# A state-space scan on one core: the output products of a group's third and fourth token block move to the projections' PSUM banks

## The chip, the cores and the metric

The kernel runs on one core of a Trainium2 chip. The metric is the device time of one execution in microseconds (us). A core has five engines with a queue of their own each: TensorE (PE in the profile, its weight loads PEld), VectorE (DVE), ScalarE (ACT), GpSimd (POOL) and SyncE (SP), which here issues the DMAs. TensorE writes its results into PSUM, which has eight banks of 2 KB for each of the 128 partitions; a tile of 128x512 numbers of 32 bits fills one bank.

## What is computed

The reference is one layer of a network on 16 sequences of 32 tokens with 512 features: a graph part, a scan part (a selective state-space layer of 128 heads in 8 groups), and a feed-forward part. The change lies in the scan part, whose reference is, cut to its core:

```
proj = einsum('bsd,od->bso', h, in_proj_w)
gate = proj[..., :D_INNER]                       # D_INNER = 8192
hBC  = silu(causal_conv(proj[..., D_INNER:...], conv_w, conv_b))
...
y  = (Y_diag + Y_off) + Dp * hid
yg = y * silu(gate)
ygr = yg.reshape(b, s, 8, 1024)
ygr = ygr * rsqrt(mean(ygr * ygr, axis=-1) + EPS)
out = einsum('bsd,od->bso', ygr.reshape(b, s, D_INNER) * gnorm_w, out_proj_w)
return residual + out
```

The 512 tokens are four blocks of 128. The 8192 inner features are eight groups of 1024, and a group is eight tiles of 128 features.

## The kernel before

The scan part (`scan_part`) holds the normalised input transposed as `hT` and goes through the groups with four functions.

- `project(t)` loads 256 KB of `in_proj` into one of six `win` buffers (L1117) and makes one 128x512 product in four matmuls of 128x128 weights (L1120), in a PSUM tile of the pool `ps_p`, tag "p". This pool has two banks, used in turn.
- `inner(g)` does this for the eight tiles of a group, twice each: the gate, `ppg`, which ScalarE's Silu carries to `gs` (L1199), and the features, `ppch`, which `convolve` carries to `hid` with one ScalarE and three VectorE instructions on the PSUM tile (L1127, L1132) and a Silu (L1135). `gs` and `hid` have two buffers each, so the projections of group g+2 write where group g's values were.
- `mix(g)` does the scan within the group, tile by tile: transposes of `hid` into `pht` (L1228), scaled by VectorE to `hd` (L1230); decays from GpSimd, TensorE and ScalarE (`da`, `pl`, `ed`, L1208 to L1218); VectorE's products `el` (L1241); the matmuls `py` (L1249); VectorE's `hid` and `gs` (L1253, L1254); ScalarE's squares and scaling (L1256 to L1261), with GpSimd adding the squares to `ssq` (L1260).
- `close(g)` ends the group. Four small matmuls `pn` sum `ssq` (L1268); from them ScalarE and VectorE make the factor `rs` (`gr` in the profile). The eight tiles `wo` of `out_proj` are loaded (L1276, ten buffers). Then, for each of the four token blocks q, eight matmuls with a 128x512 result add up in `po` (L1281), and VectorE reads `po`, scales it by `rs` and adds it to `xt` (L1284).

The eight banks are four pools of two: `ps_p` (projections), `ps_m` (`pht`, `pl`), `ps_y` (`py`, `pn`) and `ps_o` (`po`):

```
ps_p = cx.enter_context(tc.tile_pool(name="sps_p", bufs=2, space=PSUM))
ps_m = cx.enter_context(tc.tile_pool(name="sps_m", bufs=2, space=PSUM))
ps_y = cx.enter_context(tc.tile_pool(name="sps_y", bufs=2, space=PSUM))
ps_o = cx.enter_context(tc.tile_pool(name="sps_o", bufs=2, space=PSUM))
```

A pool hands its banks out in the order in which the program asks for tiles, and the first write to a tile waits until the last reader of the tile that had the bank before is done. The program asks in this order: `inner(0)`, `inner(1)`, `mix(0)`, `close(0)`, `inner(2)`, `mix(1)`, `close(1)`, and so on. The order within each engine's queue isn't the order of the text. The framework's scheduler builds it ahead of time and lets instructions that it holds for ready go before older ones that aren't. So in the built kernel the output products of the first two blocks are spread over the mix of their group, as tiles of `gs` become ready; the products of the last two follow after `pn`; and between a mix's instructions there are also the first projections of the group after the next. On TensorE, the end of group 3 in the built order reads (a number behind x counts matmuls):

```
pn3 x4, po3_0 x1, po3_1 x2, po3_2 x8, po3_3 x8, ppch40 x2, pht32 x3, ppg41 x4, ppch41 x4, ...
```

Here `ppg40` and half of `ppch40`, the first projections for group 5, stand further up, in the mix of group 3.

Of the kernel before, what the change touches and what calls it, by code (L numbers as in the profile page):

```python
# [8 lines left out]
F32 = mybir.dt.float32  # L9
# [9 lines left out]
P = 128  # L19
B = 16  # L20
C = 32
D = 512
# [1032 lines left out]
def scan_part(nc, tc, cx, I, id32, ones, xt, u, rstd, lows):  # L1055
# [6 lines left out]
# [4 lines that stand above are left out]
# [198 lines left out]
    def close(g, gs, ssq):  # L1264

        pn = ps_y.tile([P, 4], F32, tag="y", name=f"pn{g}")
        for q in range(4):
            nc.tensor.matmul(pn[:, q:q + 1], lhsT=ssq[:, q * P:(q + 1) * P], rhs=ones[:, 0:1], start=True, stop=True)  # L1268
        mean = sm.tile([P, 4], F32, tag="gm", name=f"gm{g}")
        nc.vector.tensor_scalar(mean, pn, 1.0 / (TG * P), None, ALU.mult)  # L1270
        rs = sm.tile([P, 4], F32, tag="gr", name=f"gr{g}")
        rstd(sm, rs, mean, 4, f"gn{g}")
        wo = []
        for i in range(TG):
            w = wpool.tile([P, D], F32, tag="wo", name=f"wo{g}_{i}", bufs=TG + 2)
            nc.sync.dma_start(out=w, in_=I["out_proj"][g * TG + i])  # L1276
            wo.append(w)
        for q in range(4):
            po = ps_o.tile([P, D], F32, tag="o", name=f"po{g}_{q}")
            for i in range(TG):  # L1280
                nc.tensor.matmul(  # L1281
                    po, lhsT=gs[:, i, q * P:(q + 1) * P], rhs=wo[i], start=(i == 0), stop=(i == TG - 1)
                )
            nc.vector.scalar_tensor_tensor(xt[:, q], po, rs[:, q:q + 1], xt[:, q], ALU.mult, ALU.add)  # L1284

    cur = inner(0)
    for g in range(G_M):
        nxt = inner(g + 1) if g + 1 < G_M else None
        ssq = mix(g, *cur)
        close(g, cur[0], ssq)  # L1290
        cur = nxt
# [142 lines left out]
```

## Time and profile before

| what | us |
|---|---|
| three runs | 2415.48, 2420.97, 2423.53 |
| their median | 2420.97 |
| the profiled execution's own time | 2416.21 |
| span of its trace | 2414.5 |
| TensorE busy | 2190.0 |
| VectorE busy | 1699.6 |
| matmuls of `po` (L1281), busy | 240.5 |
| matmuls of `ppg` and `ppch` (L1120), busy | 231.9 and 232.2 |
| VectorE's readout of `po` (L1284), mean of one | 0.748 |

The span runs from the first to the last instruction of the trace, and the profiled execution's time has 1.7 us around it. Busy times of TensorE are modelled ends of pipelined matmuls, so neighbours overlap by some 0.17 us in the rows and the distance of two starts tells more than a duration. A program's matmul with 32-bit operands leaves two records in the trace. The output products lie between 1586 and 2315 us; the feed-forward part follows, and starts with the layer norm of `xt`.

### The profile page before, as it was taken

The page shows a single profiled execution, that of the slowest core. Times are in us where ns is not written, and L with a number is a line of the kernel's source. Part 1 is how long each engine was busy: PE and PEld are TensorE (multiplying, and loading weights), DVE is VectorE, ACT ScalarE, POOL GpSimd, SP SyncE. Part 2 cuts the span into 40 slices and gives each one's busy share as a digit, 9 for nine tenths or more (in the row PEclk, how much of TensorE's full clock was granted, in tenths as well). Part 3 has the DMA queues.
Part 4 walks back from the last instruction along what each step waited for, and adds up shares of the span by engine and source line. Part 5 has one row for each costly group of instructions (what it writes and reads, how often), then busy time and mean ns, then how long its engine had stood idle before and what let it go on. Part 6 is the DMA issues. An engine that isn't in the chain of part 4 may idle for free. (4 is left out here: it accounts for less than half of the span.)

```text
span 2414.5 us, 88867 instructions
## 1 busy us (share of the span) xinstructions
PE 2190.0 (91%) x39234; PEld 1248.1 (52%) x39234; DVE 1699.6 (70%) x3674; ACT 1100.1 (46%) x2023; POOL 831.6 (34%) x897
## 2 busy tenths in 40 slices
PE   5699798999999778789999789999999999999979
PEld 2255455667676454567777544444444444444422
DVE  8487797888899888889999866554553625446643
ACT  6677566667665334345555322333332424333331
POOL 2165556445446565664655300020210202021200
PEclk9799899999999999999999899999999999999989
DMA  1323232132132231422211212213112121210000
GB/s 48 80 55 77 48 80 57 43 73 47 36 70 56 54 77 46 91 52 65 63 34 41 91 53 77 75 32 91 53 53 71 35 91 46 73 55 20 27 36 18
DMA packets 121625, 137.99 MB, mean 57 GB/s; under 512 B 18398, under 2 KB 79506, under 8 KB 121154
## 3 DMA queue, kind: packets, MB, share of 16 engines
q1 hardware_dynamic: 121240, 132.32, 21.9%
q8 instruction: 308, 5.05, 0.9%
q14 instruction: 77, 0.63, 0.1%
HBM read 77.02 MB, written 12.85 MB: 37 GB/s over the span
## 5 line engine op out<-in xcount | busy, mean ns | idle before, releaser
L849 POOL TENSOR_TENSOR EN<-e,rz 128x480 f32<-128x480 f32 x344 | 342.4, 995 | 554.4 <-DVE rz L847 430.1
L874 PE MATMUL u<-WA,DD 128*32 128x128 bf16 (+1 forms) x16512 | 418.6, 250 | 26.4 <-issue 26.4
L874 PEld LDWEIGHTS <-DD 128*32 128x32 f16 x16512 | 338.8, 98 | 72.7 <-issue 68.5
L879 ACT COPY us<-u 128x512 f32<-128x512 f32 x516 | 302.0, 587 | 149.5 <-PE u L874 131.8
L834 ACT ACTIVATE e<-s,smc 128x480 f32<-128x480 f32 x344 | 227.6, 662 | 290.7 <-PE s L829 248.0
L770 POOL TENSOR_TENSOR DD<-fs,crep 128x480 f16<-128x480 f32 (+2 forms) x344 | 349.6, 1017 | 0.0
L902 PEld LDWEIGHTS h<-e,us 128*32 128x32 f32 (+1 forms) x11008 | 248.8, 126 | 144.1 <-issue 65.6
L902 PE MATMUL h<-e,us 128*32 128x30 f32 (+1 forms) x11008 | 282.0, 211 | 37.1 <-DVE e L855 19.4
L821 DVE TENSOR_REDUCE c<-s 128x16 bf16<-128x480 f32 x344 | 220.7, 642 | 107.0 <-PE s L812 104.4
L1132 DVE SCALAR_TENSOR_TENSOR cyh<-ppch,t_conv_w,cyh 128x496 f32<-128x496 f32 (+2 forms) x192 | 137.4, 716 | 221.7 <-ACT cyh L1127 217.7
L1208 POOL TENSOR_TENSOR da<-lei,dA 128x512 f32<-128x512 f32 x32 | 40.6, 1269 | 611.8 <-PE pl L1213 577.5
L1281 PE MATMUL po<-wo,gs 128*128 128x512 f32 x512 | 240.5, 605 | 10.4 <-DVE xt L1284 10.3
L1120 PE MATMUL ppch<-hT,winch 128*128 128x512 f32 x512 | 232.2, 593 | 0.0
L1120 PE MATMUL ppg<-hT,wing 128*128 128x512 f32 x512 | 231.9, 593 | 0.0
L855 DVE STREAM_TRANSPOSE e<-EN 128x512 f32<-128x512 f32 x344 | 224.4, 652 | 0.0
L841 DVE TENSOR_REDUCE z<-e 128x16 f32<-128x480 f32 x344 | 219.5, 638 | 0.0
L539 ACT ACTIVATE sgn<-kd 128x512 bf16<-128x512 f32 x256 | 153.0, 598 | 56.2 <-PE kd L538 52.4
L812 PEld LDWEIGHTS <-DD 128*32 128x32 f16 x5504 | 81.7, 96 | 163.2 <-issue 129.5
L723 DVE TENSOR_SCALAR oh<-it,rank 128x512 bf16<-128x512 f16 x512 | 158.0, 368 | 7.5 <-PE pp L689 7.5
L812 PE MATMUL s<-DX,DD 128*32 128x120 f16 x5504 | 143.1, 223 | 19.6 <-DMA DX<-DD 16.2
L1120 PEld LDWEIGHTS ppch<-hT,winch 128*128 128x128 f32 x512 | 93.7, 190 | 122.7 <-issue 122.3
L1120 PEld LDWEIGHTS ppg<-hT,wing 128*128 128x128 f32 x512 | 95.8, 190 | 114.0 <-issue 114.0
(327 smaller groups left out, 2845.6 us busy)
## 6 DMA issues: line engine op xcount, KB each, us to landing
DX<-DD SPq DMA_DIRECT2D x456, 90.0 KB
wo<-in_out_proj SPq DMA_DIRECT2D x64, 256.0 KB
wing<-in_in_proj SPq DMA_DIRECT2D x64, 256.0 KB
winch<-in_in_proj SPq DMA_DIRECT2D x64, 256.0 KB
crep<-dC SPq DMA_DIRECT2D x128, 64.0 KB
dS<-so SPq DMA_DIRECT2D x32, 256.0 KB
fs<-dS SPq DMA_DIRECT2D x128, 64.0 KB
wincB<-in_in_proj SPq DMA_DIRECT2D x8, 256.0 KB
```

The lines of the kernel that those rows point to most:

```text
L770: nc.gpsimd.tensor_tensor(d[:, :, m0 - n0:n1 - n0], win, crep[:, :, m0:n1].unsqueeze(3).to_broadcast([P, 4, n1 - m0, K]), ALU.subtract,)
L812: nc.tensor.matmul(s[rh, j * 4 * QB:(j + 1) * 4 * QB].rearrange("p (b q) -> p b q", b=4), lhsT=d[:, h, c0:c0 + 32], rhs=dx[:, h, :, c0:c0 ...
L821: nc.vector.tensor_reduce(c, live["s", at, gi].rearrange("p (i q) -> p i q", q=QB), AX.X, ALU.max, negate=True)
L834: nc.scalar.activation(e, s.rearrange("p (i q) -> p i q", q=QB), AF.Exp, scale=smc)
L841: nc.vector.tensor_reduce(z, e, AX.X, ALU.add)
L849: nc.gpsimd.tensor_tensor(en[:, :, :QB], e, rz.unsqueeze(2).to_broadcast([P, NI, QB]), ALU.mult)
L855: nc.vector.transpose(e.rearrange("p i q -> p (i q)"), en.rearrange("p i q -> p (i q)"))
L874: nc.tensor.matmul(u[rh, jj], lhsT=d[:, h, c0:c0 + 32], rhs=WA[k][:, h].rearrange("p b o -> p (b o)"), start=(jj == 0 and k == 0), stop=(k ...
L879: nc.scalar.copy(us[:, j - jj:j + 1], u)
L902: nc.tensor.matmul(h[r:r + co, pr, q0:q0 + QB], lhsT=us[:, j, b * co:(b + 1) * co], rhs=e[:, 4 * j + b, :QB], start=npair > 1, stop=True, ...
L1120: nc.tensor.matmul(pp, lhsT=w[:, k], rhs=hT[:, k], start=(k == 0), stop=(k == 3))
L1281: nc.tensor.matmul(po, lhsT=gs[:, i, q * P:(q + 1) * P], rhs=wo[i], start=(i == 0), stop=(i == TG - 1))
```

## The change

`close` takes the PSUM tiles of the third and fourth token block (q = 2, 3) from `ps_p` under the tag "p", in place of `ps_o` under "o". The first and second stay where they were. Nothing else is edited.

```
         for q in range(4):
-            po = ps_o.tile([P, D], F32, tag="o", name=f"po{g}_{q}")
+            pool, tag = ((ps_o, "o"), (ps_p, "p"))[q // 2]
+            po = pool.tile([P, D], F32, tag=tag, name=f"po{g}_{q}")
             for i in range(TG):
                 nc.tensor.matmul(
                     po, lhsT=gs[:, i, q * P:(q + 1) * P], rhs=wo[i], start=(i == 0), stop=(i == TG - 1)
                 )
```

Every line from L1280 on has a number that is one higher in the changed kernel, so `po`'s matmuls are L1282 and its readout is L1285 there. The scheduler builds the queues anew for the changed program. On TensorE the end of group 3 becomes

```
pn3 x4, po3_0 x1, po3_1 x2, po3_2 x8, po3_3 x8, ppg40 x4, ppch40 x4, ppg41 x4, ppch41 x4, ...
```

and no projection stands in a mix any more. In SyncE's queue one weight load of six groups (2 to 7), the seventh of the group, stands behind the eight `wo` loads in place of ahead of them.

More of the change, by code (lines that the diff above doesn't have):

```diff
@@ L1278, in close @@
         for q in range(4):
-            po = ps_o.tile([P, D], F32, tag="o", name=f"po{g}_{q}")
+            pool, tag = ((ps_o, "o"), (ps_p, "p"))[q // 2]
+            po = pool.tile([P, D], F32, tag=tag, name=f"po{g}_{q}")
             for i in range(TG):
```

## The prediction

> **What bounds the kernel now.** I read the page's engine totals first, then the scan's stretch of TensorE's timeline, then its waits, group by group.
>
> ```profile
> PE 2190.0 (91%) x39234; PEld 1248.1 (52%) x39234; DVE 1699.6 (70%) x3674; ACT 1100.1 (46%) x2023; POOL 831.6 (34%) x897
> ...
> L1281 PE MATMUL po<-wo,gs 128*128 128x512 f32 x512 | 240.5, 605 | 10.4 <-DVE xt L1284 10.3
> ```
>
> The columns of the second line are busy time, mean ns of one, and the idle time just before them with its releaser. TensorE (PE) is the busiest engine. One matmul of the program is two records here (256 output matmuls, x512). Eight records of a projection start 3.433 us after the eight before them, so a 128x512 matmul costs 0.858 us of TensorE when they follow each other. The wait that the change can reach is the 10.3 us behind `xt`.
>
> The stretches from the end of one group's output products to the end of the next one's (groups 0, 1, 2 to 5 together, 6 and 7):
>
> ```profile
> 1577.50:1631.46 53.96, 52.42 (x243) 26.30 (x243) 32.41 (x48) 19.34 (x27) 14.61 (x10) 1.00 0.11 34
> 1631.46:1735.09 103.63, 102.09 (x367) 48.01 (x366) 50.63 (x74) 36.38 (x52) 15.62 (x11) 1.00 0.21 61
> 1735.09:2155.43 420.34, 415.31 (x1473) 193.03 (x1472) 202.15 (x296) 146.72 (x208) 59.34 (x44) 1.00 0.20 60
> 2155.43:2260.56 105.13, 98.86 (x358) 46.51 (x357) 51.58 (x74) 35.32 (x51) 16.06 (x11) 1.00 0.15 44
> 2260.56:2315.51 54.95, 50.78 (x241) 24.72 (x239) 32.22 (x50) 16.18 (x24) 11.55 (x9) 1.00 0.02 6
> ```
>
> After the stretch's length come busy PE, weight loads, DVE, ACT, POOL, then the granted clock. Up to group 5 PE idles 1.3 to 1.5 us a group (length less busy PE); in group 6 it idles 6.3. Groups 2 to 5 take 420.34 / 4 = 105.09 each. Now the same for the mix alone, group 5 and group 6:
>
> ```profile
> 2205.54:2260.56 55.02, 48.75 (x239) 24.60 (x238) 35.78 (x52) 21.37 (x29) 16.06 (x11) 1.00 0.08 25
> 2100.49:2155.43 54.94, 53.70 (x250) 26.34 (x249) 34.62 (x52) 22.73 (x30) 14.87 (x11) 1.00 0.12 32
> ```
>
> Equal lengths, yet group 5 fits in 4.95 us more of PE work. TensorE's timeline of group 5 shows what that is, and the wait at the end:
>
> ```profile
> 2102.04 1.88 PE L1120 MATMUL ppg<-hT,wing 128*128 128x512 f32 x4
> ...
> 2105.51 1.12 PE L1120 MATMUL ppg<-hT,wing 128*128 128x512 f32 x2
> ...
> 2108.12 1.02 PE L1120 MATMUL ppg<-hT,wing 128*128 128x512 f32 x2
> ...
> 2110.59 1.88 PE L1120 MATMUL ppch<-hT,winch 128*128 128x512 f32 x4
> ...
> 2137.60 2.82 PE L1281 MATMUL po<-wo,gs 128*128 128x512 f32 x6
> 2141.59 14.00 PE L1281 MATMUL po<-wo,gs 128*128 128x512 f32 x32 [1.17 <-DVE xt L1284]
> ```
>
> Twelve records, six matmuls, are projections for group 7, run in group 5's mix while the mix waits for VectorE. Group 6 has no such work, because there is no group 8. Its waits:
>
> ```profile
> PE py L1249 <- DVE el L1241: 3.7, 6, 1.4
> PE po L1281 <- DVE xt L1284: 1.2, 1, 1.2
> PE pht L1228 <- DVE hd L1230: 0.8, 1, 0.8
> PE pn L1268 <- POOL ssq L1260: 0.4, 1, 0.4
> PE pht L1228 <- ACT ed L1218: 0.2, 1, 0.2
> ```
>
> **The change part by part.** No instruction's form or count changes. `po2` and `po3` of each group leave the two "o" banks for the two "p" banks. Three things follow.
>
> (1) *The wait before `po2` goes.* It came from `po0`'s bank, which is free only when the factor `rs` is there and VectorE has read the bank. By starts: group 5's six records from 2137.60 end at 2137.60 + 6 x 0.429 = 2140.17, the next starts at 2141.59: 1.42. Group 6: 1.43. Group 0: 2 records of `ppch16` from 1615.43, then 1617.62: 1.33. Group 7: 4 records from 2297.51, then 2301.51: 2.28. Sum 1.33 + 6 x 1.42 + 2.28 = 12.1 us gained, all on the path, since PE is the chain there. The "p" bank that `po2` takes is free: its last reader, the convolution of the last projection (L1132), ran at 2209.3 in group 6, 35 us earlier. The gain's lower bound is 0, if that bank were taken after all; its upper bound is the wait itself. I take the whole wait.
>
> (2) *The projections ahead leave the mix.* The "p" pool has two banks in turn. In program order `po2` and `po3` of group g now stand between the projections of group g+1 and those of g+2, so the first two projections of g+2 can't start until `po2` and `po3` are read out. In the changed kernel's instruction order they follow `po3`, all 16 in a row. What leaves the mixes: `ppg16` (4 matmuls) and three of `ppch16` in group 0, six matmuls in each of groups 1 to 5: 37. In the open stretch each costs 0.858: 37 x 0.858 = 31.7 us. What the mix gives back for it is what the rows say: with six of them 54.94, without 55.02, so nothing. Is group 6 a fair copy? In the changed kernel the instruction order of VectorE, ScalarE and GpSimd in groups 1 to 5 is that of group 6 before, instruction for instruction, and TensorE's is too but for three or four transposes (three cost 0.33) that now stand behind the projections. The cover was VectorE's work (35.78 of 55.02 busy, most in the first 40 us) and the chain `hd`, `el`, `py`; with the fillers gone PE idles there. In group 0 the first five fillers stood while `py1` waited for `hd` (until 1583.23), so that start doesn't move. From below: group 7's mix, without convolutions, runs 2260.56 to 2315.24, less its 2.28 wait 52.40, against 55.02 - 1.43 = 53.59 for group 6; if six mixes were like that, 6 x 1.19 = 7.1 less. From above: nothing beyond 31.7. I take 31.7, as group 6 is the nearer row, and keep 24.6 for the range.
>
> (3) *Two matmuls of `po2` go ahead.* In group 0 one stands where the sixth filler stood, in group 7 one before `pn7`, where PE idles 0.92 for `ssq`. 2 x 0.86 = 1.7 us gained; bounds 0 and 1.7.
>
> SyncE's queue: in six groups (2 to 7) the seventh projection-weight load moves behind the eight `wo` loads, because its buffer is freed by the first projection. It is now issued about 3.4 us after `po3` and needed six projections later, at 20.6: 17.2 us of lead. Before, the following load had 2157.34 to about 2174.6, also 17 us, with the same burst in front (2150 to 2160) and no wait. I cost it at nothing. Behind it stand only later weights. Banks at the seam: `po2`'s readout (2253.89, 0.75 long) ends 6 us before the first projection wants the bank, `po3`'s about 1 us after `po3`, wanted 3.43 after: nothing. The Silu that empties a projection waits for `po3` in both kernels.
>
> Sum: + 31.7 - 12.1 - 1.7 = **+17.9 us**. Check by boundaries: groups 2 to 6 would take 5 x (16 x 3.433 + 55.02 + 0.33 - 1.43) = 544.2 for 525.47 (+18.8), group 1 108.85 for 103.63 (+5.2), group 0 -3.05, group 7 -3.14: +17.8. The profiled execution would go from 2416.21 to 2434.1 (span 2414.5 to 2432.4). It is 4.76 below the median of the runs; on 2420.97 that is **2438.9 us**.
>
> [...]
>
> **The rivals.** (a) *The mixes shrink when the fillers go*, and only the removed waits count: 2421.0 - 13.8 = 2407. For it: PE is 91% busy and the wait is plain. It decides once each of six mixes is 17.9 / 6 = 3.0 us shorter than group 6's. Against: group 6's 5.1 us of waits for VectorE, GpSimd and ScalarE (the list above without `xt`), with the very order that the others now get.
> (b) *The mixes are like group 7's*: +17.9 - 7.1 = +10.8, 2431.8. For: group 6's start is crowded by the last convolution. Against: in the changed order that convolution stands there in every group.
> (c) *`po2` still waits*, the change doesn't do what it says: +31.7, 2452.7. Against: the 35 us above.
> (d) *The seam stalls*, a weight arriving late behind the `wo` burst: each us costs 6; by the whole burst of 10 us it is +60, near 2499. Against: 17 us of lead.
>
> **How the numbers follow.** Forecast 0.84, (a) 0.03, (b) 0.08, (c) 0.03, (d) 0.02. The runs of before spread from 2415.48 to 2423.53. Low end: fastest run + 10.8 = 2426.3, taken as 2427. High end: slowest run + 17.9, with group 0's 3.05 not gained, 2444.5, and 1.5 for rows that differ: 2446. A measurement of this kernel can tell a change of about 0.3% (7.3 us) from none. Faster by more: (a), 0.03. Within: the parts of (a) and (b) near zero, 0.03. Slower: the rest, 0.94.
>
> **What would show it.** The wait of `po` for `xt` gone from PE's list; `py` waiting for `el` some 3 to 4 us in each of groups 1 to 6; no projections inside a mix; 16 in a row after `po3` with no gap; groups 2 to 5 at about 108.9 us each, group 7 near 51.5. Wrong if those groups stay at 105 or less, if `po` still waits for `xt`, or if projections wait at the seam.

## The result, and the profile after

Six runs of the changed kernel took 2437.02 to 2446.91 us, median 2438.96; six of the kernel before took 2412.85 to 2423.53, median 2420.39. The ratio is 1.0091, with a 95% interval of 1.0068 to 1.0114: 22 us slower (16 to 28). The ratio uses every run; the two medians alone lie 18.6 us apart. The profiled execution took 2437.02 us with a span of 2435.3, which is 20.8 us more than the one of before. The prediction of 2438.9 us and of a slower kernel held, and so did the sum's two large terms. A small one, for the clock, was missing.

The page's totals and the line of the output products, with the columns as before:

```profile
PE 2194.5 (90%) x39234; PEld 1253.2 (51%) x39234; DVE 1700.7 (70%) x3674; ACT 1098.1 (45%) x2023; POOL 834.4 (34%) x897
...
L1282 PE MATMUL po<-wo,gs 128*128 128x512 f32 x512 | 240.8, 607 | 0.2 <-ACT gs L1261 0.2
```

Same work, same counts. The idle time before `po` fell from 10.4 us to 0.2, so the wait that the change was to remove is gone. The stretches from group to group, cut at the end of each group's output products (groups 0, 1, 2, 3, 5, 6, 7; then busy PE, weight loads, DVE, ACT, POOL, and the granted clock):

```profile
1575.42:1627.53 52.11, 48.30 (x229) 24.84 (x229) 31.73 (x48) 19.34 (x27) 13.78 (x10) 0.97 0.10 31
1627.53:1737.28 109.75, 105.25 (x369) 49.94 (x368) 50.01 (x74) 36.45 (x52) 15.38 (x11) 0.98 0.19 58
1737.28:1848.40 111.12, 106.62 (x369) 50.37 (x368) 50.01 (x74) 36.44 (x52) 15.37 (x11) 0.97 0.20 57
1848.40:1957.16 108.76, 103.71 (x369) 48.87 (x368) 51.48 (x74) 36.49 (x52) 15.86 (x11) 1.00 0.20 59
...
2065.94:2174.83 108.89, 103.83 (x370) 48.87 (x368) 51.46 (x74) 36.49 (x52) 16.07 (x11) 1.00 0.20 60
2174.83:2283.61 108.78, 103.73 (x369) 48.82 (x368) 51.46 (x74) 35.20 (x51) 16.07 (x11) 1.00 0.15 43
2283.61:2335.16 51.55, 50.27 (x241) 24.80 (x239) 32.24 (x50) 16.18 (x24) 11.56 (x9) 1.00 0.02 7
```

A group lasts 108.8 us at full clock, where it lasted 105.1, and PE now idles 5.1 us in it (108.76 less 103.71) where it idled 1.3. Groups 1 and 2 are longer still, and there the clock isn't 1.00. The waits on PE over the scan, summed (us in total, times, longest):

```profile
PE py L1249 <- DVE el L1241: 21.9, 36, 1.4
PE pht L1228 <- DVE hd L1230: 4.7, 6, 0.8
PE py L1249 <- DVE hd L1230: 3.3, 1, 3.3
PE pn L1268 <- POOL ssq L1260: 2.8, 7, 0.4
```

In the kernel before, the first of these was 4.9 us, 10 times, most of it in group 6. The waits of group 6 now stand in each mix of groups 1 to 6. The seam, on PE's timeline at the end of group 5:

```profile
2158.44 16.55 PE L1282 MATMUL po<-wo,gs 128*128 128x512 f32 x38
2174.83 3.60 PE L1120 MATMUL ppg<-hT,wing 128*128 128x512 f32 x8
2178.26 3.60 PE L1120 MATMUL ppch<-hT,winch 128*128 128x512 f32 x8
```

All 38 records of the rest of `po` in one run, with no wait for `xt`, and the projections behind them with no gap.

### The profile page after: what moved, and what is told of

Same layout as the page of the kernel before. It is cut to its first block, busy times and chain, and to the rows that moved or that the text cites. A ratio compares the mean times of both kernels' runs of the same rounds, so it can differ in the third digit from the quotient of the medians.

```text
span 2435.3 us, 88884 instructions
## 1 busy us (share of the span) xinstructions
PE 2194.5 (90%) x39234; PEld 1253.2 (51%) x39234; DVE 1700.7 (70%) x3674; ACT 1098.1 (45%) x2023; POOL 834.4 (34%) x897
## 3 DMA queue, kind: packets, MB, share of 16 engines
q1 hardware_dynamic: 121240, 132.32, 21.9%
## 5 line engine op out<-in xcount | busy, mean ns | idle before, releaser
L874 PE MATMUL u<-WA,DD 128*32 128x128 bf16 (+1 forms) x16512 | 417.2, 249 | 21.3 <-issue 20.8
L1282 PE MATMUL po<-wo,gs 128*128 128x512 f32 x512 | 240.8, 607 | 0.2 <-ACT gs L1261 0.2
```

Source lines behind the costliest of these rows:

```text
L874: nc.tensor.matmul(u[rh, jj], lhsT=d[:, h, c0:c0 + 32], rhs=WA[k][:, h].rearrange("p b o -> p (b o)"), start=(jj == 0 and k == 0), stop=(k ...
L1282: nc.tensor.matmul(po, lhsT=gs[:, i, q * P:(q + 1) * P], rhs=wo[i], start=(i == 0), stop=(i == TG - 1))
```

## The experiments

Three theories stood against each other. A is that of the prediction: the change loses because the projections ahead are driven out of the mixes, and wins the removed wait. B: tiles of `po` in a foreign pool cost by themselves, at the seam. C: the loss is the clock, which in the changed kernel's trace stands at 0.50 in three stretches that follow idles of PE (the last section has them). Each run is compared with runs of the kernel before on its own chip. On the two chips used that kernel took 2410.25 and 2411.55 us (medians of 9 and 11 runs), some 10 less than the absolute figures in the expectations assume, so the ratios and differences are what to compare.

**e1, other banks.** The two tiles go to the banks of `py` and `pn`:

```
-            pool, tag = ((ps_o, "o"), (ps_p, "p"))[q // 2]
+            pool, tag = ((ps_o, "o"), (ps_y, "y"))[q // 2]
```

> po2 and po3 take the two banks of py and pn in place of the projections' banks; the projections ahead keep their places in the mix. Theory A (the change lost by driving 37 projection matmuls out of the mixes, 31.7 us, and won 12.1 us by the removed wait): only the gain is left, with one po2 matmul before pn7 another 0.9, so 13 us faster than before, near 2407. Rival B (the loss lies in the bank swap itself, any po tile in a foreign pool costs a wait at the seam to the next group): no faster than before, 2420 or more. Rival C (what the changed kernel lost is the halved clock after idle stretches): also near 2407, since PE has no idle stretch here; C is not told apart by this run.

Measured: 2400.11 us, ratio 0.9956 (0.9941 to 0.9971), 10.6 us faster than before. One group period of this run, with the columns of the stretches above:

```profile
2022.54:2126.15 103.61, 103.55 (x370) 48.33 (x370) 50.44 (x74) 36.68 (x52) 14.86 (x11) 1.00 0.19 61
```

103.61 where it was 105.09, and PE has 0.06 us of idle left. The wait is worth 1.5 us a group, and a tile of `po` in a foreign pool costs nothing when the projections keep their place. So B falls for these banks, and e3 and e4 test it for the projections' own. The same swap with another pool is a gain. It is 10.6 us (7 to 14) where 13 were expected.

**e2 and e3, one tile at a time.** In e2 only `po3`, in e3 only `po2` goes to the projections' banks:

```
-            pool, tag = ((ps_o, "o"), (ps_p, "p"))[q // 2]
+            pool, tag = (ps_p, "p") if q == 3 else (ps_o, "o")
```

(e3 has `q == 2`.)

> Only po3 goes to the projections' banks, po2 stays in the bank of po0. The built order has no projections in the mixes (as in the changed kernel), and po2 still waits for xt: the loss alone. Theory A: +31.7 less 0.9 for one po3 matmul that goes ahead in group 0, 2451, and PE waits for xt again, some 10 us in 8 waits. Rival B: half the tiles, half the loss, at most +10, near 2430. Rival C: as A for the order, but without the 31.7: a few us, as the idle stretches only cost through the clock.

> Only po2 goes to the projections' banks, po3 stays with po1. The built order on TensorE is that of the changed kernel. Theory A: the loss needs only one request in the projections' pool between two groups, so this takes as long as the changed kernel, 2437 to 2447, wait for xt gone. Rival B: half the changed kernel's loss, with the wait gone: 2425 or less.

Measured: e2 2443.85 us, ratio 1.0142 (1.0111 to 1.0173), 34 us slower; e3 2436.56 us, ratio 1.0103 (1.0076 to 1.0129), 25 us slower. e2 is the loss without the gain. PE's timeline in e2, where the output products of two groups resume:

```profile
1722.25 14.00 PE L1282 MATMUL po<-wo,gs 128*128 128x512 f32 x32 [1.17 <-DVE xt L1285]
...
2054.87 14.00 PE L1282 MATMUL po<-wo,gs 128*128 128x512 f32 x32 [1.18 <-DVE xt L1285]
```

The wait is back. The loss lies within 27 to 42 us, and the 30.9 worked out for it is inside. In the profiled execution groups 2, 5 and 6, whose clock stayed at 1.00, last 110.24 us each (from the last readout of one group to that of the next) where groups 2 to 5 lasted 105.09 before: 5.15 us more, which is six matmuls at 0.858. e3 has one tile of `po` in the projections' pool and still the whole loss of the changed kernel, within the intervals. So half the tiles don't make half the loss: what matters is that a request of `po` stands ahead of the next projections' in that pool, not how many banks it fills.

**e4, `pn` in the projections' banks.** As e1, and `pn` is made in two tiles of the projections' pool, so that something else stands ahead of the projections (VectorE reads the halves separately, one small instruction more in each group):

```
-        pn = ps_y.tile([P, 4], F32, tag="y", name=f"pn{g}")
-        for q in range(4):
-            nc.tensor.matmul(pn[:, q:q + 1], lhsT=ssq[:, q * P:(q + 1) * P], rhs=ones[:, 0:1], start=True, stop=True)
         mean = sm.tile([P, 4], F32, tag="gm", name=f"gm{g}")
-        nc.vector.tensor_scalar(mean, pn, 1.0 / (TG * P), None, ALU.mult)
+        for h in range(2):
+            pn = ps_p.tile([P, 2], F32, tag="p", name=f"pn{g}_{h}")
+            for q in (2 * h, 2 * h + 1):
+                nc.tensor.matmul(
+                    pn[:, q % 2:q % 2 + 1], lhsT=ssq[:, q * P:(q + 1) * P], rhs=ones[:, 0:1], start=True, stop=True
+                )
+            nc.vector.tensor_scalar(mean[:, 2 * h:2 * h + 2], pn, 1.0 / (TG * P), None, ALU.mult)
```

> po2 and po3 in the banks of py as in e1, but the small product pn is made in two tiles of the projections' banks. No po is in the projections' banks; the projections are out of the mixes again, since pn is asked for ahead of them. Theory A: the 31.7 us are lost again and the wait stays removed, so the changed kernel's time, near 2439. Rival B: no loss, as e1, near 2407. Rival C: as A if PE's idle stretches halve the clock, but the granted clock would have to show it: undisturbed mixes would last no longer than before.

Measured: 2431.21 us, ratio 1.0080 (1.0057 to 1.0103), 19 us slower than before and 30 slower than e1. No tile of `po` is in the projections' pool, and the changed kernel's loss is back. Two neighbouring group periods of this run:

```profile
1933.71:2043.34 109.63, 105.13 (x370) 49.94 (x370) 50.17 (x75) 36.44 (x52) 15.38 (x11) 0.98 0.18 58
2043.34:2152.14 108.80, 103.73 (x370) 48.87 (x370) 51.63 (x75) 36.49 (x52) 16.07 (x11) 1.00 0.18 58
```

The second, at full clock, has the changed kernel's 108.8 us and its 5.1 us of idle. So the clock doesn't make the loss, and C falls as its main cause. The first, with the clock at 0.98, shows what it adds: 0.8 us.

**e5 and e7, other work for the mix.** The changed kernel with its two tiles where they are. The last tile (e5) or the last two (e7) of the next group's projections are asked for after the mix, so the scheduler may lay them into it (cut to the loop over the groups):

```
         nxt = inner(g + 1) if g + 1 < G_M else None
+        if nxt:
+            fill(g + 1, *nxt, range(TG - later))
         ssq = mix(g, *cur)
+        if nxt:
+            fill(g + 1, *nxt, range(TG - later, TG))
         close(g, cur[0], ssq)
```

(`inner` now only takes the two buffers; `fill` is its loop over the given tiles; `later` is 1 or 2.)

> The changed kernel, po2 and po3 in the projections' banks, but the last tile of the next group's projections (8 matmuls, 6.9 us) is asked for after the mix in place of before it, so the scheduler can lay it into the mix, ahead of po2's request. Theory A: the mixes have room for 5.1 us again in groups 1 to 6 and 3.3 in group 0, the wait for xt stays removed: +17.9 - 6 x 5.1 - 3.3 = -16 us against the kernel before, a ratio near 0.993, and no wait of py for el left. Two VectorE convolutions in place of one then fall into a mix; if VectorE binds there, up to 2.2 us a group come back, ratio 1.000. Rival B (po tiles in the projections' banks cost by themselves): stays slower than before, ratio 1.005 or more.

> As e5 with two tiles (16 matmuls, 13.7 us) asked for after the mix. Theory A: the room in a mix is 5.1 us, and what goes beyond it is paid in full as it was outside: as e5, ratio near 0.993, not twice the gain. If a mix had more room than its idle time says, lower than e5 by up to 1.5 us a group, 10 us in all, ratio 0.989. If the extra convolutions bind VectorE in the mix, slower than e5.

Measured: e5 2394.74 us, ratio 0.9928 (0.9913 to 0.9944), 17 us faster than before; e7 2396.11 us, ratio 0.9931 (0.9915 to 0.9946). Part of a mix of e5 on PE's timeline, and the whole mix as a stretch:

```profile
2094.15 1.88 PE L1120 MATMUL ppch<-hT,winch 128*128 128x512 f32 x4
2095.96 1.09 PE L1252 MATMUL py<-el,hd 128*64 128x128 f32 x14
...
2098.40 1.12 PE L1120 MATMUL ppch<-hT,winch 128*128 128x512 f32 x2
2099.45 1.09 PE L1252 MATMUL py<-el,hd 128*64 128x128 f32 x14
```

```profile
2083.71:2139.61 55.90, 55.34 (x258) 27.60 (x257) 37.40 (x55) 28.46 (x36) 14.71 (x11) 1.00 0.12 39
```

Eight matmuls of projection (6.9 us) stand between the mix's own. The mix lasts 55.9 us, against 53.9 in the changed kernel (2120.97 to 2174.83, without them and with the wait gone as well), so they cost 2.0 and 4.8 us of them are free: the room that the idle time had announced. From the changed kernel's ratio of 1.0091 to e5's 0.9928 are some 39 us, of which the seven mixes' room is 6 x 5.1 + 3.3 = 34; the clock accounts for the rest in the traces: it cost the changed kernel some 5 us (1.0 and 2.3 in groups 1 and 2, an estimate of 1.7 in group 0), and in e5's trace it stays at 1.00 through all eight groups. One part of the expectation missed: `py` still waits for `el`, 9 times, 4.5 us in all, where none was expected. A mix of e7 as a stretch, with 16 matmuls laid in:

```profile
2068.88:2131.62 62.74, 62.18 (x273) 30.58 (x272) 39.40 (x58) 31.60 (x40) 14.67 (x11) 1.00 0.13 43
```

It is 6.84 us longer than e5's, and eight matmuls more at 0.858 are 6.86. So what goes beyond the room is paid in full, and e7 gains no more than e5.

**e6, the mix of group 6.** e1 with the last tile of group 7's projections asked for after `mix(6)`: the edit of e5, for that group alone.

> e1 with the last tile of group 7's projections asked for after mix(6): 8 matmuls are laid into the mix of group 6, the only one that had none. Theory A: 5.1 us of idle are used, so 5 us less than e1: ratio near 0.9935 against before. Rival B says nothing here. If the fillers were not free after all, as e1, 0.9956.

Measured: 2395.84 us, ratio 0.9933 (0.9919 to 0.9946). Against e1's 0.9956 that is 5.5 us less, and 5.1 were expected; the intervals of the two overlap, and e1 ran on the other chip, so the runs alone don't settle it. The traces do for this one group. Its stretch in e1, then in e6:

```profile
2126.15:2232.30 106.15, 101.59 (x359) 48.19 (x358) 50.16 (x74) 36.57 (x52) 15.38 (x11) 0.97 0.13 42
2127.24:2226.04 98.80, 98.24 (x359) 46.17 (x358) 51.14 (x74) 40.61 (x55) 14.68 (x11) 1.00 0.14 46
```

In e1 this mix ran partly at a lower clock (0.97 in its row; fourteen records of `py` at 2203.90 take 1.97 us where those at 2200.78 take 1.09), so its 106.15 us hold some 2.4 us of that: group 6 of the kernel before, 105.13 less its wait of 1.43, gives 103.7. From there to 98.80 are 4.9 us. e5, e6 and e7 can't be told apart, and each beats both the changed kernel and the one before.

## Why the prediction was right

*The wait before `po2` goes, 12.1 us.* Shown. `po` waits for `xt` no more, and e1, which has this part and one matmul of `po2` that goes ahead, takes 1.5 us less a group and 10.6 in all (7 to 14).

*The projections ahead leave the mix, 31.7 us.* Shown three ways: the changed kernel's groups at full clock last 108.8 us (108.85 worked out); e2, where the wait is back, loses 34 us (27 to 42); and e4 loses 30 against e1 without touching `po`'s use of that pool. That the fillers had been free, which the prediction read from two mixes of equal length, is what e5 then used the other way round.

*Group 6 as the copy.* Its 5.1 us of waits turned up in each mix of the changed kernel: 36 waits of `py` for `el`, 21.9 us, where the kernel before had 10 with 4.9. Rival (b), that the mixes would look like group 7's, is out: 108.8 and not 107.6.

*The seam, cost 0.* No gap between `po3` and the projections, nor among them. The weight load behind the `wo` burst, issued at 2178.46 after group 5, is in time: the seventh projection, which uses it, starts at 2195.43, 3.43 us after the sixth.

*The other rivals.* (a) needed mixes 3.0 us shorter than group 6's; they weren't. (c) is out with the wait gone. (d) with the seam.

*The sum.* By boundaries the profiled scan gave: group 0 -1.85 (-3.05 predicted), group 1 +6.1 (+5.2), groups 2 to 6 +20.9 (2283.61 less 1737.28, against 525.47; +18.8), group 7 -3.1 (-3.1; counted, as in the prediction, to 2315.24, since the row of 54.95 us ends 0.27 later, at a modelled end of a matmul), together +22.0 where +17.8 was worked out. Three places are off, by 4.2 us in all, and they are the three with a clock below 1.00. The prediction set no term for the clock. In group 0 it also misread a row: it held the start of `py1` fixed because `hd` was ready only at 1583.23. That is the end of the second of two `hd` tiles; `py1` needs the first, done at 1582.63, and started at 1583.62, when the fillers had ended, 6.12 us after the boundary; without them it started after 5.19 us (1580.61 less 1575.42). This gain of 0.9, a new wait of 0.40 for `ssq` and an estimate of 1.7 for the clock (3.41 us of work at half speed) make up the 1.2 by which group 0 is off. In the profiled executions, the scan also started 2.1 us earlier and what follows it was 0.9 longer, which makes the 20.8. That the median agreed to 0.1 us is luck: runs of one kernel spread over 10 us, the missing term is 4, and the change itself is known no closer than 16 to 28 us.

*The explanation of the banks* was too narrow. The prediction had the projections wait until both tiles are read out of both banks. e3 shows that one request is enough to drive out all of the projections, and the built order of e4 that even a tile read long before `po` ends does it. In all these built orders the order of requests in the pool decides, and one tile of `po` drives out as much as two. A pool with more banks was not tried.

## What to carry to other kernels

A PSUM bank that stands free isn't free if the next stage's work asks the same pool after you: where a scheduler grants a pool's tiles in the order of requests, as it did in the built orders here, a tile lent to another user pushes back everything asked for behind it, and work that filled idle time goes with it (e3: one tile, 25 us). Before moving a tile, look for a stage of the same kernel that already runs without the filler, as group 6 did here; its length is the price, and it needs no model. Then look for a pool whose next request comes late (e1), or give the idle stretch other work by asking for it later in the program (e5).

## What the runs showed of the hardware

The clock fell in three mixes: behind an idle of PE of 3.29 us in group 0, and in groups 1 and 2 where no single idle was over 1.36 us. Three stretches of the changed kernel with their granted clock (the column before the last two):

```profile
1694.00:1697.40 3.40, 3.40 (x16) 2.39 (x17) 2.54 (x5) 2.72 (x4) 1.27 (x1) 0.50 0.00 0
1803.30:1810.10 6.80, 6.37 (x20) 3.42 (x20) 4.75 (x9) 3.82 (x6) 1.88 (x2) 0.50 0.01 2
1581.40:1584.80 3.40, 3.40 (x13) 1.94 (x10) 1.44 (x2) 1.33 (x2) 0.81 (x1) 0.50 0.02 5
```

13.6 us at half clock, in the mixes of groups 1, 2 and 0; the kernel before had none in its profiled scan (1.00 in every stretch of 100 us or less from 1577 to 2315.5). PE's timeline at the second:

```profile
1800.61 1.09 PE L1249 MATMUL py<-el,hd 128*64 128x128 f32 x14 [0.57 <-DVE el L1241]
1801.96 0.40 PE L1249 MATMUL py<-el,hd 128*64 128x128 f32 x2 [0.26 <-DVE el L1241]
1803.73 1.97 PE L1249 MATMUL py<-el,hd 128*64 128x128 f32 x14 [1.36 <-DVE el L1241]
1805.63 2.08 PE L1282 MATMUL po<-wo,gs 128*128 128x512 f32 x2
```

Fourteen records of `py` take 1.97 us where they take 1.09 above, and two of `po` 2.08 for 1.12 (group 5, at 2133.50). The idles ahead of it are 0.57, 0.26 and 1.36 us. The same pattern in group 6 of the kernel before, with a longest idle of 1.37, kept its clock at 1.00, as it did in groups 3 to 6 here. e1's group 6, with 0.58, 0.26 and 1.37, has records of 1.97 us again (2203.90). So idles that agree to 0.01 us stood ahead of a clock of 0.50 in some mixes and of 1.00 in others. What decides between the two is not shown: no experiment here varied the idles alone.

The half clock costs time beyond the idle: groups 1 and 2, at 0.98 and 0.97, lasted 1.0 and 2.3 us longer than the 108.8 of those at 1.00. It may be a part of why the changed kernel's runs go up to 2446.91: the two longest had a granted clock of 0.966 and 0.967, the other four 0.969 to 0.972.
